# Input statistics of images 1 to 3: from VectorE's bn_stats to ScalarE accumulator passes about the first tile's mean

## The chip, the cores and the metric

The kernel runs on one core of one Trainium2 chip. The metric is device time in microseconds (us) of one execution. The engines are named as in the profile: PE (TensorE; PEld its weight loads), DVE (VectorE), ACT (ScalarE), POOL (GpSimd) and SP (SyncE, which here only issues DMAs). Each engine works through its own instructions in the order in which they were written; between engines, semaphores make one wait for another.

## The reference

Input x has 4 images of 512 channels on 64 x 64 places. Two layers follow each other, each with a group norm (32 groups of 16 channels, statistics over a whole image) ahead of it and a residual around it:

- Layer 0, a Mamba block: a layer norm over channels, the channels cut into 4 chunks of 128, for each chunk projections, a 4-tap convolution, silu, softplus, and a state scan over all 4096 places with 256 inner channels and 16 states, then an output projection, a second layer norm, and a 512 x 512 projection.
- Layer 1, linear attention with 8 heads: relu of queries and keys, key-query products summed over all places, and output projections.

The part that matters here is the mean and variance that the first group norm needs:

```
m = jnp.mean(g, axis=(2, 3, 4), keepdims=True)
s = jnp.var(g, axis=(2, 3, 4), keepdims=True)
return ((g - m) / jnp.sqrt(s + eps)).reshape(v.shape)
```

They take one pass over an image before its first tile can be normed. Per channel the kernel gathers mean and variance, and a small matmul with a matrix of groups (`stats_end`, L344) makes group figures of them.

## The kernel before, in words

An image has 8 tiles of 512 places; a tile holds 4 blocks of 128 channels x 512 places, 1 MB in float32. The main loop goes over 128 steps, one for each image, tile and chunk, and each step has 16 slots: 2 halves of the inner channels, 4 groups of states, and 2 halves of a group. In one slot (`slot`, L741):

- DVE runs two scans (L755), each over 512 places, that read a decay `dA` and an input `bx`.
- ACT computes the decays of later scans (`decay`, L724: one exp each, written to one of three PSUM banks, `LEAD = 3`, so the decay of scan k + 3 waits until scan k is done).
- POOL computes the inputs `bx` of the slot after next (`drive`, L733; three buffers, so it waits for the scans of the slot before).
- In odd slots POOL also copies the last state (L766) and multiplies the last quarter of the states with the output weights (L767); in the following slot DVE does the other three quarters (`product`, L772, traced as L775) and PE sums over states.

Around that, at fixed slots of each step, ACT has bursts: at slot 3 softplus between two loads of activation tables (L1147, L636, L1149), at slot 10 silu between two (L1066, L1067, L1169); and POOL has a gate multiply at slots 1 and 9 and a larger one at slot 4 (L797, L644).

All other work is cut into pieces, Python generators that yield after each piece, and put into four queues. `ahead` holds the norm of the next tile, `late` the end of a finished tile, `rest` the attention of the image before, and `light` the statistics of the next image's input (`input_norm(b + 1)`, added at an image's first step). Image 0's statistics are taken before the loop. At the end of each slot the loop decides what of each queue goes in (L1172 to 1200). `light` gets a turn only in the slots `AWAY = (3, 10)`, or when it waits:

```
if light and light[0][1] == "wait" or s in AWAY and not any(
    q and q[0][1] == "wide" for q in (ahead, late)
):
    one(light)
```

`stats0` (L810) loads a tile of x (names `xs`), then in each turn puts two `bn_stats` on DVE (L816, one per block), so a tile takes one turn for its load and two for its blocks. At the end four `bn_aggr` (L341) give mean and variance. `one` (L1076) lets a queue's next piece run if the word that it yielded is among those allowed in this slot.

Tiles of x, of the finished layer 0 and of attention share three buffers of 1 MB (`TILES = 3`); whoever wants one while all are held yields "wait". Loads are issued on SP's queue, together with all rows that the scans need.

The second group norm's statistics are already gathered in the manner that the change brings: `shifted` (L559) takes bn_stats of the first tile, and for the 7 others lets ACT pass over each block twice (L575), Identity with the negative mean of the first tile as bias, and Square with the same bias, each with an accumulator that sums the outputs; `shifted_end` (L581) makes mean and variance of the sums. Each pass writes its full output to a buffer that nobody reads.

Of the kernel before, what the change touches and what calls it, by code (L numbers as in the profile page):

```python
# [10 lines left out]
AF = mybir.ActivationFunctionType  # L11
# [13 lines left out]
def kernel(  # L25
# [311 lines left out]
    def aggregate(stats, name):  # L337

        mv = small.tile([P, NC, 2], F32, tag="mv", name=f"mv_{name}", bufs=4)
        for c in range(NC):  # L340
            nc.vector.bn_aggr(mv[:, c, :], stats[:, c, :, :].rearrange("p t s -> p (t s)"))  # L341
        return mv

    def stats_end(mv, name):  # L344

        yield from room()
        pm = work_bank(f"pm_{name}")
        mm(pm[:, 0:NC], grp, mv[:, :, 0], start=True, stop=True)
        yield from pause(1)
        ngm = small.tile([P, NC], F32, tag="ngm", name=f"ngm_{name}", bufs=4)  # L350
        nc.vector.tensor_scalar(ngm, pm[:, 0:NC], -1.0, None, ALU.mult)
        d = pm[:, 2 * NC : 3 * NC]
        nc.vector.tensor_tensor(d, mv[:, :, 0], pm[:, 0:NC], ALU.subtract)
        dev = small.tile([P, NC], F32, tag="dev", name=f"dev_{name}")
        nc.vector.tensor_tensor(dev, mv[:, :, 0], pm[:, 0:NC], ALU.subtract)
        nc.vector.tensor_tensor(d, dev, d, ALU.mult)
        nc.vector.tensor_tensor(dev, d, mv[:, :, 1], ALU.add)
        pv = pm[:, NC : 2 * NC]
        mm(pv, grp, dev, start=True, stop=True)
        yield from pause(1)  # L360
        gr = small.tile([P, NC], F32, tag="gr", name=f"gr_{name}", bufs=4)
        nc.vector.tensor_scalar(gr, pv, 1e-5, None, ALU.add)
        free()
        nc.gpsimd.tensor_tensor(gr, gr, mhalf, ALU.pow)
        off = small.tile([P, NC], F32, tag="off", name=f"off_{name}", bufs=4)
        nc.gpsimd.tensor_tensor(off, ngm, gr, ALU.mult)
        return gr, off, ngm
# [439 lines left out]
    def with_skip(f, xn, c):  # L807
        nc.scalar.copy(xn[:, c, NTAP - 1 : NTAP - 1 + T], f["po"])

    def stats0(stats, b):  # L810

        for t in range(NT):
            xt = yield from load_x(b, t, "s")
            yield
            for c in range(NC):
                nc.vector.bn_stats(stats[:, c, t, :], xt[:, c, :])  # L816
                if c == NC - 1:
                    later(1, free_x)
                if c % 2:
                    yield "wait" if c == NC - 1 else None  # L820
# [213 lines left out]

    def input_norm(b):
        stats = stats_tile(f"st0_{b}")
        yield from stats0(stats, b)
        norms[b] = yield from stats_end(aggregate(stats, f"a{b}"), f"a{b}")
        yield

    def tile_norm(b, t):
# [34 lines left out]
    def one(queue, may=ANYWHERE):  # L1076

        while queue:  # L1080
            if queue[0][1] not in (None, "wait", "more", "free") and queue[0][1] not in may:
                return False
            queue[0][1] = next(queue[0][0], queue)
            if queue[0][1] is not queue:
                return queue[0][1] != "wait"
            queue.pop(0)
        return False
# [26 lines left out]
    with tc.manual_schedule():  # L1114
        credit, seen, mix, held[0], held_x[0] = 0.0, work["mm"], iter(()), 0, 0
        for n, (b, t, c) in enumerate(steps):
            f, nm = fs[n], names[n]
            before = fs[n - 1] if n else None
            nxt = fs[n + 1] if n + 1 < N else None
            front = step_inputs(n + 2) if n + 2 < N else iter(())  # L1120
            last_mix, mix = mix, mixers(fs[n + 2], names[n + 2]) if n + 2 < N else iter(())
            if c == 0 and (t + 1 < NT or b + 1 < B):
                add_to(ahead, tile_norm(b, t + 1) if t + 1 < NT else tile_norm(b + 1, 0))
            if c == 0 and t == 0 and b + 1 < B:
                add_to(light, input_norm(b + 1))
            assert c != 2 or not ahead
            for s in range(SLOTS):
                def after():
                    nonlocal credit, seen
                    now[0] = n * SLOTS + s  # L1130
                    for what in [w for at, w in due if at <= now[0]]:
                        what()
                    due[:] = [d for d in due if d[0] > now[0]]
                    if s == 0 and before is not None:
                        take_y(before, n - 1, 1)
                    if s == SLOTS // 2:
                        take_y(f, n, 0)
                    if s < 2:
                        next(last_mix, None)
                    if s < 4:  # L1140
                        spread(f, 1, nm, s)
                    if s == 1 and before is not None:
                        gate(before, 1)
                    if s == 2 and nxt is not None:
                        time_banks(nxt, names[n + 1])
                    if s == 3 and nxt is not None:
                        nc.scalar.preload_act_table_set("softplus")  # L1147
                        time_steps(nxt, names[n + 1])
                        nc.scalar.preload_act_table_set("natural_log_exp_and_others")  # L1149
                    if s == 6 and before is not None:  # L1150
                        pb_, pt_, pc_ = steps[n - 1]
                        with_skip(before, xn[pb_, pt_], pc_)
                        if pc_ == NC - 1:
                            add_to(late, leave(pb_, pt_))
                    if s in (3, 5, 6, 7, 8, 9):
                        next(front, None)
                    if s == 4 and nxt is not None:
                        to_rows(nxt, 0, names[n + 1])
                        to_rows(nxt, 1, names[n + 1])
                    if s == 4 and before is not None:  # L1160
                        pb_, pt_, pc_ = steps[n - 1]
                        out_proj(before, xn[pb_, pt_], pc_, names[n - 1])
                    if s == 9:
                        gate(f, 0)
                    if 8 <= s < 12 and nxt is not None:
                        spread(nxt, 0, names[n + 1], s - 8)
                    if s == 10 and n + 2 < N:
                        silu(n + 2)
                        nc.scalar.preload_act_table_set("natural_log_exp_and_others")  # L1169
                    if s >= 12:  # L1170
                        next(mix, None)
                    may = [  # L1172
                        what for k, what in ((0, "wide"), (1, "one ahead"), (2, "two ahead"))
                        if any(a - 2 * k <= s <= a - k for a in AWAY) or (k == 2 and s == SLOTS - 1)
                    ]
                    if light and light[0][1] == "wait" or s in AWAY and not any(
                        q and q[0][1] == "wide" for q in (ahead, late)
                    ):
                        one(light)

                    limit[0] = 1 if 0 < s < 6 else 2
                    credit = min(credit + 3.5 - (work["mm"] - seen), 2.6)
                    busy = False
                    for queue in (ahead, late, rest):
                        kind = queue[0][1] if queue else None
                        if queue is ahead or kind == "free" or credit > 0 or kind == "more" and not busy:
                            start = work["mm"]
                            one(queue, ANYWHERE if queue is ahead and (c, s) > (1, 4) else may)
                            credit -= work["mm"] - start
                            busy = busy or work["mm"] - start > 1  # L1190
                    if s - 1 in AWAY:
                        for queue in (ahead, late, rest):
                            if queue and queue[0][1] == "free":
                                one(queue)
                    seen = work["mm"]

                slot(n * SLOTS + s, N * SLOTS, after)
            fs[n - 1].clear() if n else None
        product(N * SLOTS - 1)
        fold_states(N * SLOTS - 1, N * SLOTS)  # L1200
        now[0] = None
        for _, what in due:
            what()
# [60 lines left out]
```

## Time and profile before

| what | value |
|---|---|
| median of 3 runs | 7839.31 us (7833.92 to 7841.01) |
| the profiled execution's own time | 7841.1 us |
| its span, first to last instruction | 7839.4 us |
| busy in the span: DVE, POOL | 6905.7 us, 6898.4 us (88% each) |
| busy in the span: PE, ACT | 6444.4 us (82%), 5461.7 us (70%) |
| bn_stats of x (L816) | 128, 81.1 us busy, 32 of them before the loop |
| accumulator passes already there (L575) | 224 and as many reads of the accumulator |

The loop runs from 121 to 7364 us of the span; what follows is the last image's attention, mainly on PE. A busy share is a mean over stages with different limits, so it doesn't tell what a shorter stretch of work is worth: for that one looks at what each engine waits for at that place. In the chain of work that ended last, a step goes back from each instruction to what released it. In the lists of waits, a wait for several things is put down to the one that came last.

### The profile page before, as it was taken

What the parts mean: (1) busy time and instruction counts of PE and PEld (TensorE: products, weight loads), DVE (VectorE), ACT (ScalarE), POOL (GpSimd) and SP (SyncE); (2) the same over time, 40 slices, a digit from 0 to 9 for tenths busy, and PEclk for the clock granted to TensorE, in tenths of its full rate; (3) what the DMA queues carried; (4) which work ended last, traced back from release to release, by engine and by line L of the source; (5) the groups of instructions that cost most, each with busy time, mean ns of one, the idle gap of its engine ahead of it and who ended that gap; (6) DMA issues with size and microseconds to landing.
All of it is one profiled execution on the core that took longest, in us unless ns stands there. A gap on an engine that the chain in (4) does not pass through costs nothing.

```text
span 7839.4 us, 90421 instructions
## 1 busy us (share of the span) xinstructions
PE 6444.4 (82%) x24839; PEld 2099.0 (27%) x24880; DVE 6905.7 (88%) x5650; ACT 5461.7 (70%) x8329; POOL 6898.4 (88%) x4649
## 2 busy tenths in 40 slices
PE   5677777677789888988788888898788888989599
PEld 1121212112223222322222223332222222323144
DVE  5999999999999999999999999999999999999500
ACT  4677777777777777777777777777777777777421
POOL 4999999999999999999999999999999999999500
PEclk7888878888899999998899999999899999999799
DMA  5666666666666656776666666676666666586302
GB/s 164 165 172 168 158 150 162 162 157 169 174 179 169 159 159 159 192 197 169 174 166 169 167 162 160 171 190 183 164 160 168 157 162 154 148 212 182 100 33 91
DMA packets 829184, 1265.87 MB, mean 161 GB/s; under 512 B 183912, under 2 KB 317560, under 8 KB 816384
## 3 DMA queue, kind: packets, MB, share of 16 engines
q1 hardware_dynamic: 804736, 1222.32, 59.6%
q0 software_dynamic: 16896, 33.56, 2.5%
q8 instruction: 195, 3.19, 0.2%
q10 hardware_dynamic: 7040, 4.20, 0.2%
q14 instruction: 317, 2.60, 0.1%
HBM read 1052.78 MB, written 206.57 MB: 161 GB/s over the span
## 4 chain that ended last, share of the span: by engine, by line
DVE 33%; PE 31%; ACT 10%; issue 8%; DMA 7%; POOL 7%; SPq 3%; POOLq 0%; DVEq 0%; ACTq 0%
DVE h L755 21%; DVE h L775 10%; PE pq L129 6%; PE y L129 6%; PE pc L129 5%; POOL bx L737 5%; ACT dA L729 4%; DMA d_all<-d_rows 3%; PE pr L129 3%; PE po L129 2%; SPq L704 2%; PE pp L129 2%; DMA c_sb<-c_rows 2%; PE pd L129 1%; DMA b_all<-b_rows 1%
## 5 line engine op out<-in xcount | busy, mean ns | idle before, releaser
L737 POOL TENSOR_TENSOR bx<-d_all,b_all 128x1024 f32<-128x1024 f32 x2048 | 4824.0, 2367 | 198.2 <-DVE h L755 178.6
L755 DVE TENSOR_TENSOR_SCAN h<-dA,st,bx 128x512 f32<-128x512 f32 x3584 | 4355.5, 1265 | 292.5 <-PE y L129 101.8
L729 ACT ACTIVATE dA<-d_all,a_t 128x512 f32<-128x512 f32 x4096 | 2759.0, 688 | 1491.5 <-DVE h L755 1434.8
L775 DVE TENSOR_TENSOR h<-h,c_all 128x1536 f32<-128x1536 f32 x1024 | 1768.6, 1727 | 0.1
L767 POOL TENSOR_TENSOR h<-h,c_sb 128x512 f32<-128x512 f32 x1024 | 1299.8, 1269 | 99.1 <-DMA c_sb<-c_rows 13.0
L129 PE MATMUL y<-h,fold 128*32 128x512 f32 x8192 | 1264.0, 693 | 45.7 <-POOL h L767 42.4
L129 PE MATMUL c_all<-parts,sel 128*128 128x384 bf16 x1024 | 369.4, 361 | 1021.9 <-DVE h L775 1020.7
L129 PE MATMUL pc<-xn,w_cv 128*128 128x512 f32 x2048 | 1036.6, 639 | 126.0 <-DVE xn L421 62.2
L129 PE MATMUL pq<-w_qk,xa 128*128 128x512 f32 x2048 | 962.5, 602 | 6.7 <-issue 4.1
L755 DVE TENSOR_TENSOR_SCAN h<-dA,bx 128x512 f32<-128x512 f32 x512 | 590.1, 1204 | 76.6 <-ACT dA L729 46.5
L129 PEld LDWEIGHTS pc<-xn,w_cv 128*128 128x128 f32 x2048 | 386.4, 199 | 735.6 <-issue 409.3
L129 PEld LDWEIGHTS <-sel 128*128 128x128 bf16 x1280 | 126.8, 99 | 1668.0 <-DVE h L775 1453.4
L129 PEld LDWEIGHTS pq<-w_qk,xa 128*128 128x128 f32 x2048 | 395.7, 195 | 437.4 <-issue 421.7
L129 PE MATMUL pp<-xn,w_pr 128*128 128x512 f32 x1024 | 478.0, 597 | 3.8 <-DVE xn L421 3.8
L129 PE MATMUL pr<-xb,m 128*128 128x512 f32 x1024 | 476.1, 603 | 4.8 <-POOL m L992 2.2
L129 PE MATMUL y<-xz,dg 32*32 32x512 f32 x2048 | 362.1, 785 | 0.0
L129 PEld LDWEIGHTS y<-h,fold 128*32 128x32 f32 x8192 | 170.5, 114 | 639.7 <-issue 398.1
L848 ACT ACTIVATE kq<-pq 128x512 f32<-128x512 f32 x256 | 150.8, 589 | 265.5 <-PE pq L129 264.8
L797 POOL TENSOR_TENSOR xz<-xz 128x512 f32<-128x512 f32 x256 | 325.1, 1270 | 10.2 <-ACT xz L794 9.3
L644 POOL TENSOR_TENSOR dt<-dt,xz 128x1024 f32<-128x1024 f32 x128 | 302.1, 2360 | 21.4 <-ACT dt L636 21.4
L855 DVE TENSOR_TENSOR kq<-pk,kq 128x256 f32<-128x256 f32 x124 | 51.2, 413 | 277.9 <-PE pk L129 277.7
L129 PE MATMUL pd<-xz,w_xp 128*128 128x512 f32 x512 | 289.3, 692 | 5.2 <-ACT xz L1066 5.2
(178 smaller groups left out, 6164.7 us busy)
## 6 DMA issues: line engine op xcount, KB each, us to landing
d_all<-d_rows SPq DMA_DIRECT2D x2048, 256.0 KB, 4.3
b_all<-b_rows SPq DMA_DIRECT2D x4096, 64.0 KB, 2.3
d_rows<-dt SPq DMA_DIRECT2D x256, 512.0 KB, 2.7
c_sb<-c_rows SPq DMA_DIRECT2D x4096, 16.0 KB, 3.5
xs<-in_x_dram SPq DMA_DIRECT2D x32, 1024.0 KB, 7.8
xn<-in_x_dram SPq DMA_DIRECT2D x32, 1024.0 KB, 8.4
xr<-in_x_dram POOLq DMA_DIRECT2D x32, 1024.0 KB, 10.2
x<-xr SPq DMA_DIRECT2D x32, 1024.0 KB, 4.5
```

Source lines behind the costliest of these rows:

```text
L129: nc.tensor.matmul(out_, lhsT, rhs, **how)
L644: nc.gpsimd.tensor_tensor(f["both"][:, 1], f["both"][:, 0], f["xz"][:, 0], ALU.mult)
L704: nc.sync.dma_start(dst[k * BLK : (k + 1) * BLK, :], rows_[q * KS + k, :].partition_broadcast(BLK))
L729: nc.scalar.activation(dAs[k], fs[n]["d_all", e][:, 0, j, :], AF.Exp, scale=a_t[:, e, j, q : q + 1])
L737: nc.gpsimd.tensor_tensor(bxs[g], fs[n]["d_all", e][:, 1, jj * 2 : jj * 2 + 2, :], bc(b_all[g // JJ], 2), ALU.mult)
L755: nc.vector.tensor_tensor_scan(h[:, j, :], dAs.pop(2 * g + i), bxs[g][:, i, :], 0.0 if t == 0 else st[:, c, e, q, j : j + 1], ALU.mult, AL ...
L767: nc.gpsimd.tensor_tensor(h[:, :, CUT:], h[:, :, CUT:], bc(c_sb.pop(g // JJ), NJ), ALU.mult)
L775: nc.vector.tensor_tensor(own, own, bc(c_all.pop(g // JJ), NJ), ALU.mult)
L797: nc.gpsimd.tensor_tensor(f["xz"][:, 1, e, :], f["xz"][:, 1, e, :], f["xz"][:, 0, e, :], ALU.mult)
L848: nc.scalar.activation(qk[i], pq, AF.Relu)
L855: nc.vector.tensor_tensor(kq, pk, kq, ALU.add)
```

## The change

For images 1 to 3 a new `stats_by_act` takes the place of `stats0`. The first tile still gets one bn_stats per block, whose mean and variance seed the sums. For the other seven tiles each block gets two ACT passes: Identity with the negative mean of the first tile as bias, written back in place, and Square of what that wrote, again in place; each with an accumulator output. `shifted_end`, which was there already, makes mean and variance of the sums. All small results live in the tile that held the bn_stats.

A block is one piece, and yields the word "row". The loop no longer gives such a piece a turn in the slots 3 and 10, but in slots 0, 2, 8 and 14, one block in each. Loads of a tile keep the old turns.

```diff
+    def stats_by_act(stats, b):
...
+        for t in range(NT):
+            xt = yield from load_x(b, t, "s")
+            yield "row"
+            for c in range(NC):
+                if t == 0:
+                    nc.vector.bn_stats(first[:, c, :], xt[:, c, :])
+                    if c == NC - 1:
+                        for o in range(NC):
+                            nc.vector.bn_aggr(mv[:, o, :], first[:, o, :])
+                        nc.scalar.activation(off[:, :, 0], mv[:, :, 0], AF.Copy, scale=-1.0)
+                        nc.vector.memset(sums[:, :, 0:1], 0.0)
+                        nc.scalar.activation(squares[:, :, 0], mv[:, :, 1], AF.Copy, scale=float(T))
+                else:
+                    nc.scalar.activation(
+                        xt[:, c, :], xt[:, c, :], AF.Identity, bias=off[:, c, :],
+                        accum_out=sums[:, c, t : t + 1],
+                    )
+                    nc.scalar.activation(
+                        xt[:, c, :], xt[:, c, :], AF.Square, accum_out=squares[:, c, t : t + 1]
+                    )
+                if c == NC - 1:
+                    later(1, free_x)
+                yield "row" if c < NC - 1 else None
+        return {"sum": sums, "square": squares, "mv": mv}
...
     def input_norm(b):
         stats = stats_tile(f"st0_{b}")
-        yield from stats0(stats, b)
-        norms[b] = yield from stats_end(aggregate(stats, f"a{b}"), f"a{b}")
+        if b:
+            sums = yield from stats_by_act(stats, b)
+            mv = shifted_end(sums, f"a{b}")
+        else:
+            yield from stats0(stats, b)
+            mv = aggregate(stats, f"a{b}")
+        norms[b] = yield from stats_end(mv, f"a{b}")
         yield
...
-                    if light and light[0][1] == "wait" or s in AWAY and not any(
+                    turn = light and light[0][1]
+                    if turn == "wait" or turn != "row" and s in AWAY and not any(
                         q and q[0][1] == "wide" for q in (ahead, late)
                     ):
                         one(light)
+                    elif turn == "row" and s in (0, 2, 8, 14):
+                        one(light, ("row",))
```

## The prediction

> **What bounds the kernel now.** I read the busy times first, then the groups, then the waits, then stretches of equal work, and last one step engine by engine.
>
> The page's first part, and the groups (line, engine, operation, output<-inputs, count | busy us, mean ns | idle us before, releaser):
>
> ```profile
> PE 6444.4 (82%) x24839; PEld 2099.0 (27%) x24880; DVE 6905.7 (88%) x5650; ACT 5461.7 (70%) x8329; POOL 6898.4 (88%) x4649
> ...
> L737 POOL TENSOR_TENSOR bx<-d_all,b_all 128x1024 f32<-128x1024 f32 x2048 | 4824.0, 2367 | 198.2 <-DVE h L755 178.6
> L755 DVE TENSOR_TENSOR_SCAN h<-dA,st,bx 128x512 f32<-128x512 f32 x3584 | 4355.5, 1265 | 292.5 <-PE y L129 101.8
> L729 ACT ACTIVATE dA<-d_all,a_t 128x512 f32<-128x512 f32 x4096 | 2759.0, 688 | 1491.5 <-DVE h L755 1434.8
> ```
>
> DVE and POOL are equally busy; ACT idles 1491 us ahead of its dA, nearly all of it waiting for a scan to free a bank. So ACT has time, but in pieces. The waits (who for whom, us, times, longest) show that DVE and POOL seldom wait long for each other:
>
> ```profile
> POOL bx L737 <- DVE h L755: 178.6, 296, 3.4
> POOL st L766 <- DVE h L755: 58.1, 61, 4.5
> ...
> DVE h L755 <- ACT dA L729: 140.4, 103, 44.5
> ```
>
> Next, steps 1 to 13 of images 1, 2 and 3, bounded by the starts of their scans. Images 1 and 2 hold 32 of the bn_stats each, image 3 none; scans, tile norms and attention of the image before are the same in all. First all engines, then L816 alone:
>
> ```profile
> 1926.00:2667.30 741.30, 631.69 (x2557) 204.00 (x2563) 712.24 (x608) 552.75 (x842) 700.71 (x474) 0.93 0.67 171
> 3754.80:4500.40 745.60, 637.87 (x2557) 206.21 (x2563) 711.95 (x609) 553.00 (x842) 700.23 (x474) 0.92 0.66 170
> 5587.80:6334.80 747.00, 629.85 (x2560) 205.15 (x2566) 693.50 (x567) 552.85 (x841) 700.04 (x472) 0.93 0.63 160
> ...
> 1926.00:2667.30 741.30, 20.34 (x32) 0.93 0.67 171
> 5587.80:6334.80 747.00, 0.00 (x0) 0.93 0.63 160
> ```
>
> (Columns: length, busy us and count of PE, PEld, DVE, ACT, POOL.) Image 3 has 18.5 us less on DVE and is not shorter: the time went into waits. In image 0 (172 to 773 us) DVE is busy 592 and POOL 589 of 601 us. The loop hangs on both engines by turns: by the starts of copy L766 and of bx, POOL is 1 to 3 us behind DVE from slot 3 to about 8 (gate, dt), and in most steps of images 1 to 3 has caught up at slots 13 to 1.
>
> **The Trainium skill.** "ScalarE: Activation LUTs", section What ACT_TABLE_LOAD costs: an ACTIVATE with a pointer bias takes 280 + 0.833 N ns, 707 at N = 512; following ones overlap by 93 ns. The trace has 704 to 733 ns for L575, the same form, and starts 0.63 us apart. "Perfetto Trace Analysis", section Optimizing Scalar/DVE Operations: if DVE is saturated, moving work to Scalar may make sense; its section Optimization Strategy says that the contended engine can change over time. The windows agree with the second; whether the first applies is the question here.
>
> **The change, part by part.**
> *DVE.* Three images times 7 tiles times 4 blocks are 84 bn_stats fewer. Each lasts 0.677 us, but a pair holds the engine for 1.20 (261.90 to 263.09 below), so 84 x 0.60 = 50 us. bn_aggr: 12 of 0.315 become 12 of 0.149 (minus 2.0); six reduces of 0.17 and small work add 1.2. Net minus 51 us.
> *ACT.* 84 blocks. L575's two passes and their accumulator reads run 2526.98 to 2528.40 before the next dA, 1.42 us. Here the Square reads what Identity wrote and waits for its end, about 0.08 more, since a dependent pair (L414, L415) has 0.03 us between end and start: 1.5 us, 126 in all. Bounds: 1.42 with no such wait, 1.8 with nothing overlapped (0.71 + 0.19, twice).
> *POOL.* The end of the sums adds 0.25 + 3 x 0.20 = 0.85 us per image, 2.5 in all, on an engine that is 98% busy in image 0 (589 of 601 us).
> *SP.* The same 24 loads of 1 MB, now mostly at slot 10, once a step. They land in 5.6 to 11.8 us; the first block is at slot 14, about 13 us later. Nothing else in the queue is added; d_all's spreads share the wires with it, as before. Cost nothing; if a load came later, all of ACT's queue, dA first, would stand behind the block.
> *PE.* Nothing. Pieces of attention in steps 1 to 13 of images 1 and 2 move by some slots, because the tile buffers change hands earlier.
>
> *Blocks at slots 0, 2 and 14 (63).* Behind them ACT idles for DVE: 1.9 us in slot 1, 2.1 in slot 3, 1.4 and 1.1 in slots 14 and 15 (means over the steps). Walking each block down ACT's queue until idle time has used it up, and comparing with the scan that takes each dA, 0.3 us in all is late at slot 14, nothing at slot 0, 3.8 at slot 2, where softplus and two table loads follow. POOL is behind there. I take plus 2.
>
> *Blocks at slot 8 (21).* Step 2, ACT, then DVE, then POOL; the block goes in after the second line:
>
> ```profile
> 256.54 0.67 ACT L606 ACTIVATE xz<-pc,cb 128x512 f32<-128x512 f32 x1
> 257.11 0.57 ACT L794 COPY xz<-y 128x512 f32<-128x512 f32 x1
> 257.58 1.31 ACT L729 ACTIVATE dA<-d_all,a_t 128x512 f32<-128x512 f32 x2
> 258.81 0.59 ACT L623 COPY xz<-pz 128x512 f32<-128x512 f32 x1
> ...
> 260.25 1.73 DVE L775 TENSOR_TENSOR h<-h,c_all 128x1536 f32<-128x1536 f32 x1
> 261.90 1.28 DVE L816 BATCH_NORM_STATS2 st<-xs 128x6 f32<-128x512 f32 x2
> 263.09 3.59 DVE L755 TENSOR_TENSOR_SCAN h<-dA,bx 128x512 f32<-128x512 f32 x3
> ...
> 262.94 4.67 POOL L737 TENSOR_TENSOR bx<-d_all,b_all 128x1024 f32<-128x1024 f32 x2
> ```
>
> The dA of 257.58 moves to 259.08 and is done at 259.77, so the scan that started at 259.14 starts 0.7 later and the product at 260.9 ends at 262.7. The pair of bn_stats is gone, so slot 11 starts at 262.6, 0.5 earlier. Slot 12 needs bx, which POOL ends at 265.3, so it starts at 265.4 against 265.46. The block's 1.5 is paid by the pair's 1.2 and by slack. The other 20 go the same way; at the end of their steps DVE stands from 0.9 us early to 1.2 late (steps 5 and 9, where a pair goes and no block comes, counted in): plus 4.6 us summed. About half is met by a POOL that is behind anyway: plus 2.5.
>
> *The 19 pairs removed at slot 3.* DVE's 1.2 us are mostly gone by slot 8, where it waits for POOL or PE: minus 3, between 0 and minus 10.
>
> Sum: 2 + 2.5 - 3 + 2.5 = plus 4. The profiled execution took 7841.1 (span 7839.4 and 1.7 around it), so 7845; the median shown is 1.8 below it, so 7843.
>
> **The rivals.** What a measurement of this kernel can tell from no change is 0.2%, 15.7 us.
> *DVE is the bound where it counts (faster).* For it: from slot 9 to slot 1 POOL's copy often follows the scan at once. If all 29 pairs at slot 10 pay 1.2 (34.8), the 12 first-tile bn_stats in other slots cost 7.2 and POOL 2.5, the gain is 25: 7814. Against: image 3's 747 us, and the silu burst after slot 10 (1.28 + 1.48 + 0.58 + 1.28), which a pair covers.
> *The silu burst comes late (slower).* A slot-8 block pushes the dA behind that burst. With the scans kept at their places, 21 blocks make dA 0.92 us late on average: 19.3, slot 2 adds 3.8 and POOL 2.5: plus 26, 7867. It decides once the missing pair no longer pays, that is, where DVE's early time at slot 10 is lost to POOL. Against: about 2526 us, two L575 blocks stand ahead of the burst and DVE shows no idle time, under a pair and a kq.
> *Only the order of attention changes.* The same work took 741 and 745.6 us in images 1 and 2, so 4 us an image, 8 in all, of either sign; this fills the first case's own range.
> That the change doesn't act is excluded: in the built order, all 84 pairs stand at slots 0, 2, 8 and 14.
>
> **How the numbers follow.** Balance 0.57, 7843, own range 7828 to 7858 (attention's 8, and 1.42 or 1.8 us for a block). Faster 0.26 at 7814. Slower 0.17 at 7867. The range runs from 7808 to 7868: it takes in both rivals and leaves some 0.1 on each side for more. Faster, within and slower have the same chances as the cases.
>
> **What would show it.** Right: bn_stats of xs fall from 128 to 44 with DVE's busy time some 50 us lower; two new ACT groups of 84 at 0.71 us each with reads of 0.19; DVE's idle time before L755 up by about as much as its work fell; POOL's idle time hardly moved. Wrong if POOL's idle for DVE falls by 20 us or more (faster), or if DVE's wait for ACT dA in slots 10 to 12 grows by over 20 (slower); and if the Square starts over 0.3 us after Identity's read, the block is mis-sized.

## The result, and the profile after

The changed kernel takes 7862.95 us (median of 8 executions, 7855.59 to 7871.39) against 7840.16 for the kernel before (median of 8, 7833.92 to 7846.71). The ratio is 1.0027, 95% interval 1.0018 to 1.0037: slower, by 21 us at this ratio. The forecast was no change, 7843, with 7867 for the slower rival.

First the busy times and the groups of the profile after (group columns as before: count | busy us, mean ns | idle us before, releaser):

```profile
PE 6462.9 (82%) x24880; PEld 2106.5 (27%) x24880; DVE 6862.0 (87%) x5575; ACT 5570.6 (71%) x8671; POOL 6901.0 (88%) x4661
...
L737 POOL TENSOR_TENSOR bx<-d_all,b_all 128x1024 f32<-128x1024 f32 x2048 | 4824.5, 2367 | 200.1 <-DVE h L755 182.8
L755 DVE TENSOR_TENSOR_SCAN h<-dA,st,bx 128x512 f32<-128x512 f32 x3584 | 4359.1, 1264 | 331.8 <-ACT dA L729 118.3
L729 ACT ACTIVATE dA<-d_all,a_t 128x512 f32<-128x512 f32 x4096 | 2749.4, 687 | 1387.1 <-DVE h L755 1339.2
```

DVE works 44 us less than before (6905.7) and stands idle ahead of these scans 39 us more (331.8 against 292.5), and 13 us more ahead of the 512 scans of each image's first tile, which are a group of their own (89.7 against 76.6). So all that was taken off it became waiting, and some more.

The new work, in the groups with each shape apart:

```profile
L832 ACT ACTIVATE xs<-xs,st 128x512 f32<-128x512 f32 x84 | 60.5, 720 | 0.4
L836 ACT ACTIVATE xs<-xs 128x512 f32<-128x512 f32 x84 | 52.9, 630 | 2.6
L832 ACT ACTIVATION_READ_ACCUMULATOR xs<-xs,st 128x1 f32 x84 | 16.0, 190 | 0.0
...
L850 DVE BATCH_NORM_STATS2 st<-xs 128x6 f32<-128x512 f32 x32 | 20.1, 680 | 0.1
L824 DVE BATCH_NORM_STATS2 st<-xs 128x6 f32<-128x512 f32 x12 | 8.0, 665 | 0.0
```

And one block as it lies in ACT's queue (start us, length us):

```profile
231.71 0.71 ACT L832 ACTIVATE xs<-xs,st 128x512 f32<-128x512 f32 x1
232.32 0.19 ACT L832 ACTIVATION_READ_ACCUMULATOR xs<-xs,st 128x1 f32 x1
232.54 0.63 ACT L836 ACTIVATE xs<-xs 128x512 f32<-128x512 f32 x1
233.08 0.19 ACT L836 ACTIVATION_READ_ACCUMULATOR xs<-xs 128x1 f32 x1
233.17 1.28 ACT L729 ACTIVATE dA<-d_all,a_t 128x512 f32<-128x512 f32 x2
```

The next dA starts 1.46 us after the block does; over all 84 blocks the median from a block's start to ACT's next instruction is 1.475. The waits (us, times, longest):

```profile
DVE h L755 <- ACT dA L729: 174.3, 145, 44.5
DVE h L755 <- PE y L129: 140.6, 137, 3.2
...
POOL bx L737 <- DVE h L755: 182.8, 298, 3.4
...
POOL st L766 <- DVE h L755: 61.4, 60, 4.8
```

DVE waits 34 us more for ACT's dA (140.4 before) and 24 us more for PE's y (116.5 before); the single wait of 44.5 us stands in both kernels ahead of the loop. POOL's idle time for DVE hardly moved (178.6 and 58.1 before).

Last the same steps as before, 1 to 13 of images 1, 2 and 3 (length, busy us and count of PE, PEld, DVE, ACT, POOL; the granted clock is the third figure from the end):

```profile
1935.94:2683.00 747.06, 632.93 (x2560) 205.21 (x2561) 697.03 (x582) 589.88 (x957) 702.91 (x480) 0.93 0.67 169
3771.92:4519.35 747.43, 632.08 (x2560) 205.76 (x2561) 696.82 (x581) 589.66 (x957) 703.08 (x480) 0.93 0.67 169
5608.35:6355.32 746.97, 630.26 (x2565) 205.23 (x2566) 693.32 (x566) 552.85 (x841) 700.07 (x472) 0.93 0.64 160
```

Images 1 and 2 lost 15 us of DVE's work and gained 37 of ACT's, and took 747 us where they took 741.3 and 745.6. Image 3, which has no such work, took 747.0 in both. From the start of the first scan to the end of the last the loop takes 7259.4 us against 7242.8 before. The work ahead of it and after it is the same in both; in these two profiles the first scan starts at 124.7 and 120.8 us, which is 4 of the 21 us between their spans.

### The profile page after: what moved, and what is told of

The parts are those of the page before. It is cut to its first block, busy times and chain, and to the rows that moved or that the text cites. A ratio compares the mean times of both kernels' runs of the same rounds, so it can differ in the third digit from the quotient of the medians.

```text
span 7860.0 us, 90717 instructions
## 1 busy us (share of the span) xinstructions
PE 6462.9 (82%) x24880; PEld 2106.5 (27%) x24880; DVE 6862.0 (87%) x5575; ACT 5570.6 (71%) x8671; POOL 6901.0 (88%) x4661
## 4 chain that ended last, share of the span: by engine, by line
PE 32%; DVE 31%; ACT 12%; DMA 7%; issue 7%; POOL 7%; SPq 2%; POOLq 0%; DVEq 0%; ACTq 0%
DVE h L755 20%; DVE h L775 10%; PE y L129 6%; PE pq L129 6%; PE pc L129 6%; POOL bx L737 5%; ACT dA L729 4%; PE pr L129 3%; DMA d_all<-d_rows 3%; PE po L129 3%; PE pp L129 2%; DMA c_sb<-c_rows 2%; SPq L704 2%; PE c_all L129 1%; DVE xn L421 1%
## 5 line engine op out<-in xcount | busy, mean ns | idle before, releaser
L755 DVE TENSOR_TENSOR_SCAN h<-dA,st,bx 128x512 f32<-128x512 f32 x3584 | 4359.1, 1264 | 331.8 <-ACT dA L729 118.3
L129 PE MATMUL y<-h,fold 128*32 128x512 f32 x8192 | 1260.6, 691 | 41.3 <-POOL h L767 37.4
L755 DVE TENSOR_TENSOR_SCAN h<-dA,bx 128x512 f32<-128x512 f32 x512 | 591.4, 1203 | 89.7 <-ACT dA L729 56.0
```

What stands on the lines that cost most here:

```text
L129: nc.tensor.matmul(out_, lhsT, rhs, **how)
L755: nc.vector.tensor_tensor_scan(h[:, j, :], dAs.pop(2 * g + i), bxs[g][:, i, :], 0.0 if t == 0 else st[:, c, e, q, j : j + 1], ALU.mult, AL ...
```

## The experiments

Three things happen at once in the change: bn_stats leave DVE, passes enter ACT, and the order of everything in the queues moves, since blocks now take one slot each, a tile is loaded and given back at other places, and pieces of the norm and of attention that wait for a tile buffer move with it. The experiments take these apart. All ratios are to the kernel before on the same chip, with 95% intervals; "loop" is the span of the scans in one profiled execution, which moves by some us between executions. "Clock" is the share of full TensorE clock that was granted over an execution, as the median of a run's executions; it turns out to matter.

| run | order | passes on ACT | us, median | ratio | clock | loop us |
|---|---|---|---|---|---|---|
| before | before | none (bn_stats) | 7837 to 7841 | | 0.906 | 7242.8 |
| after | new | 0, 2, 8, 14 | 7862.95 | 1.0027 [1.0018, 1.0037] | 0.9065 | 7259.4 |
| e1_no_passes | new | left out | 7855.10 | 1.0020 [1.0013, 1.0028] | 0.903 | 7263.5 |
| e2_without_8 | new, slots 0, 2, 14 | 0, 2, 14 | 7856.97 | 1.0028 [1.0017, 1.0038] | 0.903 | 7263.6 |
| e3_without_2 | new, slots 0, 8, 14 | 0, 8, 14 | 7899.26 | 1.0083 [1.0066, 1.0099] | 0.9005 | 7283.5 |
| e4_slots_0_14 | new, slots 0, 14 | 0, 14 | 7845.86 | 1.0011 [1.0002, 1.0020] | 0.905 | 7245.8 |
| e5_bn_out | before | left out | 7841.25 | 1.0001 [0.9993, 1.0010] | 0.906 | 7242.7 |
| e6_bn_in_rows | new | none (bn_stats, one a slot) | 7878.59 | 1.0054 [1.0037, 1.0070] | 0.9025 | 7273.0 |
| e7_before_turns | before | 0, 2, 8, 14 (5 at 10) | 7880.13 | 1.0048 [1.0033, 1.0063] | 0.9035 | 7280.1 |
| e8_passes_at_away | before | two at a time at 3, 10 | 7916.57 | 1.0099 [1.0084, 1.0114] | 0.902 | 7319.3 |
| e9_no_first_tile | new | left out, first tile too | 7848.01 | 1.0016 [1.0009, 1.0022] | 0.904 | 7239.4 |
| e10_no_loads | new | as e9, loads of x too | 7852.48 | 1.0020 [1.0010, 1.0030] | 0.902 | 7252.7 |
| e11_third_pass | new | three a block | 7880.25 | 1.0060 [1.0047, 1.0073] | 0.906 | 7287.0 |
| e12_before_turns_not_8 | before | 0, 2, 14 | 7842.92 | 1.0005 [0.9996, 1.0013] | 0.907 | 7245.8 |

### The passes left out, and other sets of slots

e1 keeps the new order, with the first tile's bn_stats, and issues no passes:

```diff
                 else:
-                    nc.scalar.activation(
-                        xt[:, c, :], xt[:, c, :], AF.Identity, bias=off[:, c, :],
-                        accum_out=sums[:, c, t : t + 1],
-                    )
-                    nc.scalar.activation(
-                        xt[:, c, :], xt[:, c, :], AF.Square, accum_out=squares[:, c, t : t + 1]
-                    )
+                    pass
```

> The changed kernel with its 84 pairs of ACT passes left out (tiles are still loaded and held for the same turns; the statistics of images 1 to 3 are then those of their first tile). Measure: the loop, from the start of the first scan to the end of the last, 7242.8 us before and 7259.4 after. Theory A, the bn_stats on DVE were worth little and the ACT passes cost: the loop is 0 to 10 us shorter than before, so the passes cost 17 to 27. Theory B, the removal pays well and the passes cost still more: 20 to 40 us shorter than before. Theory C, the passes are not the cause, but the moved loads and pieces of attention are: the loop stays 8 us or more longer than before.

The ratio stays at 1.0020. Without a single pass, 124 us of ACT's queue, three quarters of the loss are there. That it is the same loss doesn't follow: e1's executions had a lower granted clock (0.903) than those of the kernel before and of the changed kernel. "What in the order costs" comes back to this.

e2, e3 and e4 change the list of slots:

```diff
-                    elif turn == "row" and s in (0, 2, 8, 14):
+                    elif turn == "row" and s in (0, 2, 14):
```

(`(0, 8, 14)` in e3, `(0, 14)` in e4.)

> Blocks in slots 0, 2 and 14 only, so that a tile takes longer and the passes last to step 16. If the blocks at slot 8, ahead of the silu burst, cost most (theory A1): the loop falls to within 4 us of before. If those at slot 2, ahead of the softplus burst, do (A2): it stays 12 us or more longer, and slot 5 still grows by 12 or more in sum. C: unchanged from the changed kernel within 4 us.

> Blocks in slots 0, 8 and 14 only. A1: the loop stays 10 us or more longer than before, slot 11 grows as in the changed kernel. A2: it falls to within 4 us of before and slot 5 no longer grows. C: unchanged from the changed kernel within 4 us.

> Blocks in slots 0 and 14 only, in 14 steps of each image. If both early slots are to blame and the rest is hidden (A): the loop is 0 to 10 us shorter than before, as without any passes. If passes cost wherever they are put (84 times a share of 1.5 us): as long as the changed kernel, within 4 us.

Without slot 8 the time is the same as with it, without slot 2 it is 0.56% longer (a step then has three slots, so tiles are held longer), and with slots 0 and 14 alone it comes closest to the kernel before, but isn't below it. If each slot had a price of its own, taking slot 2 away could not cost 44 us. So these runs show that a list of slots is also a choice of order, and can't be read as a price list. The clock differs too: e2 and e3 have 0.903 and 0.9005.

### The bn_stats left out, in the order before

e5 is the kernel before, with the bn_stats of tiles 1 to 7 left out in images 1 to 3; PE, ACT, POOL and SP have before's instructions in before's order.

```diff
-                nc.vector.bn_stats(stats[:, c, t, :], xt[:, c, :])
+                if t == 0 or b == 0:
+                    nc.vector.bn_stats(stats[:, c, t, :], xt[:, c, :])
```

> The kernel before with the bn_stats of tiles 1 to 7 of images 1 to 3 left out and nothing else changed (statistics of those images from their first tile alone): every load and every piece of attention stays where it was. Loop before: 7242.8 us; without passes but in the changed order: 7263.5. Theory M, the moved loads and pieces of attention cost: the loop is 7235 to 7246, so removal pays next to nothing and the new order costs the 20 us. Theory R, taking the bn_stats away itself costs, since DVE then runs into other waits: 7255 or more. Rival of both, removal pays and the order costs twice as much: under 7225.

The ratio is 1.0001, at most 0.07% faster. In the same stretches of images 1 and 2:

```profile
1926.10:2665.75 739.65, 635.35 (x2562) 205.69 (x2563) 696.76 (x581) 552.11 (x842) 700.81 (x474) 0.92 0.68 171
3754.63:4495.30 740.67, 635.33 (x2562) 205.89 (x2563) 696.81 (x581) 552.41 (x842) 699.53 (x474) 0.92 0.68 171
```

and in the groups of its page:

```profile
L755 DVE TENSOR_TENSOR_SCAN h<-dA,st,bx 128x512 f32<-128x512 f32 x3584 | 4363.7, 1270 | 317.8 <-ACT dA L729 105.3
```

DVE's work falls by 15 us in each, and the stretches by 1.6 and 4.9. Summed over all steps, and with a slot running from one scan start to the next pair's, slots 3 and 10 get 12.4 and 28.4 us shorter, as they must, and slots 5, 7, 11 and 12 get 14.0, 5.4, 14.6 and 5.4 longer: the next slots in which DVE waits for POOL, ACT or PE take it back. In this order nothing was to be gained on DVE.

### The new order with bn_stats

e6 has the new order, and one bn_stats per block in place of the passes, as many as before in all.

```diff
+                nc.vector.bn_stats(stats[:, c, t, :], xt[:, c, :])
-            sums = yield from stats_by_act(stats, b)
-            mv = shifted_end(sums, f"a{b}")
+            yield from stats_by_act(stats, b)
+            mv = aggregate(stats, f"a{b}")
```

> The changed kernel's order, with one bn_stats on DVE in place of each block's two ACT passes. M: the loop is 7255 to 7275, as long as or longer than the changed kernel, since the order is the same and DVE has its work back at slots 0, 2, 8 and 14. R: at most 7248, since the bn_stats are back. If passes at ACT were what costs: at most 7248 as well.

It takes 1.0054. Slots 0, 2, 8 and 14 are 14.5, 12.6, 14.9 and 13.7 us longer than in the kernel before, for 24 bn_stats each: at 0.60 us, 14.4 us, the whole of it. In these slots DVE sets the pace, and a bn_stats costs what it lasts; in slots 3 and 10, where the kernel before puts it, it costs nothing (e5). That holds for the change too, since it keeps the first tile's 12.

### The passes in the order before

e7 keeps before's loads, its giving back of tiles and PE's and SP's order, and puts the passes at the same slots as the change; five blocks that had no slot in time stand at slot 10.

```diff
+                    elif blocks and s in (0, 2, 8, 14) and blocks[0][0] <= now[0]:
+                        _, what, k = blocks.pop(0)
+                        what(k)
```

> The changed kernel's passes in slots 0, 2, 8 and 14 (five of 84 blocks at slot 10), with the loads and the release of the tiles in the turns of before, so that the loads and all of PE's work stand as before. M: the loop is 7240 to 7250, within 4 us of the kernel without bn_stats in that order plus at most 7 for the passes. If the passes cost by themselves (the 2.5 and 2 us of the prediction were too small): 7255 or more.

e8 puts two blocks at a time where the pairs of bn_stats stood, at slots 3 and 10:

```diff
-            yield "row"
+            yield
...
-                yield "row" if c < NC - 1 else None
+                if c % 2:
+                    yield "wait" if c == NC - 1 else None
```

> The passes in the old turns, two blocks at a time in slots 3 and 10, ahead of the softplus and the silu burst; loads and PE's work stand as before. If ACT's passes are hidden wherever they are: 7240 to 7250. If a block ahead of a burst makes dA late, as the prediction's rival says: two blocks are 3 us each time, 42 times, of which at least a quarter shows: 7275 or more.

Here the passes do cost: 37 us in e7 over e5 (1.0048 over 1.0001), 77 in e8. Against e5, slot 5 is 19.0 us longer in e7 and slot 10 16.7, the slots behind those with blocks at 2 and 8. In e8 slot 5 is 31.6 longer and slot 12 35.0.

e12 is e7 without the blocks at slots 8 and 10:

```diff
                         _, what, k = blocks.pop(0)
-                        what(k)
+                        if s != 8:
+                            what(k)
```

> The order before with passes at slots 0, 2, 14 alone: the 21 blocks at slot 8 and the 5 at slot 10, ahead of and behind the silu burst, are left out, so their statistics are missing. With all 84 blocks this order took 7880, with none 7841. If half of the 37 us is the silu burst coming late (17 us by the slots 10 to 12 of the trace): 7861 to 7865. If slot 2 ahead of softplus carries all: 7878. If slot 8 carries all: 7843.

The time is back at 1.0005: without these 26 blocks 34 of the 37 us are gone. Of the 34.3 us between the two loops, 15.9 are in slot 10 and 3.9 in slot 11. Another 11.0 are in slot 5, which has the same blocks ahead of it in both; there the granted clock, 0.9035 in e7 and 0.907 in e12, may have its part. One of the blocks, at step 11 of image 1, in ACT's queue of e7, and the scan that waits (the timelines of ACT and DVE):

```profile
2542.56 0.67 ACT L606 ACTIVATE xz<-pc,cb 128x512 f32<-128x512 f32 x1
2543.13 0.57 ACT L794 COPY xz<-y 128x512 f32<-128x512 f32 x1
2543.59 0.73 ACT L825 ACTIVATE xs<-xs,st 128x512 f32<-128x512 f32 x1
...
2544.45 0.63 ACT L829 ACTIVATE xs<-xs 128x512 f32<-128x512 f32 x1
...
2545.08 0.71 ACT L575 ACTIVATE sum<-xr,moff 128x512 f32<-128x512 f32 x1
...
2546.49 1.28 ACT L729 ACTIVATE dA<-d_all,a_t 128x512 f32<-128x512 f32 x2
```

```profile
2544.47 1.28 DVE L755 TENSOR_TENSOR_SCAN h<-dA,st,bx 128x512 f32<-128x512 f32 x1
2547.19 1.28 DVE L755 TENSOR_TENSOR_SCAN h<-dA,st,bx 128x512 f32<-128x512 f32 x1 [1.44 <-ACT dA L729]
```

and the same place in e12:

```profile
2526.37 0.73 ACT L575 ACTIVATE sum<-xr,moff 128x512 f32<-128x512 f32 x1
...
2527.79 1.29 ACT L729 ACTIVATE dA<-d_all,a_t 128x512 f32<-128x512 f32 x2
```

```profile
2527.26 2.53 DVE L755 TENSOR_TENSOR_SCAN h<-dA,st,bx 128x512 f32<-128x512 f32 x2
```

Here the end of a tile already puts an accumulator block (L575) between the xz copy and the two dA. With it alone the scan of slot 10 follows at once; with a second block ahead of it the scan waits 1.44 us, the block's whole length. In steps 1 to 13 of image 1 seven blocks stand at slot 8, and slot 10 is longer in e7 than in e12 by 0, 0.5, 1.4, 0.5, 1.4, 1.5 and 0.5 us. The 1.4 to 1.5 are this step and two in which the xz copy (L794) ahead of the block waits 0.95 and 2.2 us for PE's y. A late y alone doesn't decide it: in the first and the fourth of the seven the copy waits 0.81 and 1.12 us, and slot 10 grows by 0 and 0.5. What a block costs differs from step to step, and in the step shown it is another block that has used up ACT's lead. The mean, 0.83 us, is near the 0.92 that the slower rival had worked out. In the step shown it is paid at the second scan of slot 10, by the two dA right behind the block, ahead of the silu burst and its table load.

### A third pass

e11 is the changed kernel, with one more accumulator pass in each block.

```diff
+                    nc.scalar.activation(
+                        xt[:, c, :], xt[:, c, :], AF.Identity,
+                        accum_out=squares[:, c, t : t + 1],
+                    )
                     nc.scalar.activation(
                         xt[:, c, :], xt[:, c, :], AF.Identity, bias=off[:, c, :],
```

> The changed kernel with a third accumulator pass in every one of the 84 blocks (an Identity in place, about 0.72 us each, 60 us of ACT more). If the passes are hidden in this order, as the small step from no passes to two says: not over 10 us above the changed kernel, 7863 to 7873. If they cost as in the order before (37 us for 126 us of ACT): 18 us more, 7881. If each us of ACT ahead of the bursts counts in full at slots 2 and 8 (42 x 0.72): 30 us more, 7893.

It takes 1.0060, 0.33% or 26 us over the changed kernel. The third pass costs 26 us at a like clock (0.906 and 0.9065), close to the 30 of the expectation that counts every us at slots 2 and 8. The first two passes of a block add 5 us to e1's median (1.0027 over 1.0020, the intervals overlap), but at a higher clock than e1 had. Slot 5 is 17.9 us longer and slot 10 13.4. The stretches and the waits of e11:

```profile
1935.47:2696.90 761.43, 641.13 (x2560) 206.57 (x2561) 697.65 (x582) 609.80 (x1013) 703.77 (x479) 0.92 0.65 166
3784.13:4540.14 756.01, 638.16 (x2560) 205.79 (x2561) 697.48 (x581) 609.29 (x1013) 703.23 (x480) 0.92 0.65 167
...
DVE h L755 <- ACT dA L729: 198.9, 151, 44.5
```

The third pass is paid where e7's blocks are, behind slots 2 and 8. In the changed kernel, too, slot 10 is 17.2 us longer than in e1; but slot 11 is 17.8 us shorter. The new order has a wait in slot 11 of its own (in e1 it is 15.4 us longer than in e5), and the late slot 10 runs into that wait. In e7, which lacks it, slot 11 gives nothing back.

### What in the order costs

e9 is e1 without the first tile's bn_stats and bn_aggr; e10 is e9 without the loads of x. All other instructions keep their order on every engine.

```diff
-                    nc.vector.bn_stats(first[:, c, :], xt[:, c, :])
                     if c == NC - 1:
-                        for o in range(NC):
-                            nc.vector.bn_aggr(mv[:, o, :], first[:, o, :])
+                        nc.vector.memset(mv, 1.0)
```

```diff
-            xt = yield from load_x(b, t, "s")
+            while no_tile():
+                yield "wait"
+            held_x[0] += 1
             yield "row"
```

> The new order without the passes (7855 against 7837 before), and now also without the first tile's 12 bn_stats and 12 bn_aggr: one small memset stands where they stood, so no statistics of x are taken in images 1 to 3 at all. Every other instruction keeps its place on every engine. Theory A, the 12 single bn_stats in slots 8, 14, 0 and 2 are what the new order costs: back to 7842 or less. Theories B (the loads of x at slot 10) and C (the shifted order of the norm's and attention's pieces on PE): 12 x 0.6 = 7 us at most come back, 7848 to 7855.

> The kernel of e9 with the 24 loads of x for images 1 to 3 left out as well; the tile buffers are still taken and given back at the same places, so all other engines keep e9's order. Theory B, the loads' new place in SP's queue and on the wires costs time: 10 us or more below e9. Theory C, the order of the pieces: within 4 us of e9, and the loop still some 15 us above that of the order before.

The first tile gives back little: 1.0016 for 1.0020, with overlapping intervals. Its own slots 0, 2, 8 and 14 are 8.2 us shorter in e9 than in e1, about what its 12 bn_stats at 0.60 to 0.68 and the bn_aggr take, so it does pay there; whether all of that reaches the end is not settled. Without the loads the ratio doesn't fall either (1.0020). So a kernel with no statistics of x in its loop and no loads for them is still 0.16 to 0.20% slower in its median than the kernel before, where e5, with as little to do, is not. What remains is the order of the pieces, and what comes with it: a lower granted clock, 0.904 in e9 and 0.902 in e10 against 0.906.

The profiled execution of e9 was shorter than its median (7837.9, the median 7848.0) and that of e10 was at its median (7852.2), and this shows how the clock enters. From image 1, step 5, first e9, then e10, PE's timeline:

```profile
2158.41 1.13 PE L129 MATMUL pt<-dt,w_dt 32*128 32x512 f32 x4
2160.43 1.98 PE L129 MATMUL pc<-xn,w_cv 128*128 128x512 f32 x4 [0.89 <-DVE xn L421]
2162.34 1.06 PE L129 MATMUL mu_sums_b<-xn,ones 128*32 128x512 f32 x8
```

```profile
2163.39 2.08 PE L129 MATMUL pt<-dt,w_dt 32*128 32x512 f32 x4
2166.18 3.78 PE L129 MATMUL pc<-xn,w_cv 128*128 128x512 f32 x4 [0.72 <-DVE xn L421]
2169.89 1.94 PE L129 MATMUL mu_sums_b<-xn,ones 128*32 128x512 f32 x8
```

ACT in e10, and DVE in e9 and e10, some 14 to 17 us later:

```profile
2179.91 0.69 ACT L606 ACTIVATE xz<-pc,cb 128x512 f32<-128x512 f32 x1 [1.64 <-PE pc L129]
```

```profile
2174.27 1.28 DVE L755 TENSOR_TENSOR_SCAN h<-dA,st,bx 128x512 f32<-128x512 f32 x1 [1.15 <-PE y L129]
```

```profile
2182.86 1.28 DVE L755 TENSOR_TENSOR_SCAN h<-dA,st,bx 128x512 f32<-128x512 f32 x1 [2.96 <-ACT kq L877]
```

The granted clock over the four pc (it is the third figure from the end), and over the 3.41 us ahead of the next stretch at half clock in each profile, e9 and then e10:

```profile
2160.43:2162.41 1.98, 1.98 (x8) 1.00 0.41 120
2151.06:2154.47 3.41, 0.58 (x2) 1.00 0.93 209
```

```profile
2166.18:2169.96 3.78, 3.77 (x8) 0.50 0.43 125
2158.57:2161.98 3.41, 1.52 (x13) 1.00 0.60 158
```

The same matmuls in the same order run at half their rate in e10, from pt to mu_sums_b, because half the clock is granted there (2161.98 to 2172.22 us). In e9 the half clock comes earlier and is over before pt (2154.47 to 2157.89). PE's later pieces follow without a pause, so the next pc comes late for ACT, whose copy of it stands ahead of two dA, and the scan waits 2.96 us in place of 1.15. Steps 5 and 9 of images 1 and 2 in all 14 kernels' profiles are 56 such places: where these four pc ran at full rate (0.62 us of busy time each, granted clock 1.00) slot 7 took 3.58 to 3.60 us, where at half rate (1.02 to 1.10 us, clock 0.50 to 0.56) it took 5.06 to 5.39, without exception. At how many of the four places it happens differs: 2 in the kernel before and in the changed one, 4 in e1, e2, e7 and e10, 0 in e5. It is 3.8 us of the 13 between the loops of e9 and e10, 7 of the 21 between e5 and e1, and 5 of the 34 between e12 and e7. It makes no difference between the profiles of before and after.

How far the clock alone moves the time is seen in image 3. All 14 kernels have the same instructions in the same order there, on every engine. Its steps 1 to 13 took 747.0 us in seven of the profiles, all at a granted clock of 0.93, and 748.9 to 751.0 us in the other seven, all at 0.92. The slowest is e5's:

```profile
5583.45:6334.47 751.02, 634.22 (x2565) 206.28 (x2566) 693.84 (x567) 553.08 (x841) 701.10 (x472) 0.92 0.65 159
```

Whole executions show it too: of the 85 of the kernel before in its three series, the 24 with a clock of 0.905 or less took 7840.7 us in the median, the 20 with 0.908 or more 7831.7. Of e9's 21 executions, the seven with 0.903 or less took 7853.7, the four with 0.905 or more 7837.2, which is the time of the kernel before. (A slow execution could also be the cause of a low mean; the 56 places show one way in which the clock comes first.) And e9's profile, with a clock of 0.907, shows no loss from the order in images 1 and 2, though a few us may hide behind the somewhat higher clock:

```profile
1923.02:2662.57 739.55, 628.39 (x2560) 204.23 (x2561) 694.17 (x577) 553.51 (x845) 703.33 (x480) 0.93 0.67 171
3751.54:4492.14 740.60, 631.67 (x2560) 204.37 (x2561) 694.76 (x578) 553.46 (x845) 702.76 (x480) 0.93 0.66 171
```

The changed kernel has PE's order of e9, but not the low clock of e1, e9 and e10. So their 12 to 16 us are not shown to be a part of its 21. From e9's profile to the changed kernel's, images 1 and 2 grow by 7.5 and 6.8 us, at a clock of 0.93 in both. Slot 10 grows by 12.2 us and slot 11 shrinks by 12.7; what is left is mainly slot 5, behind the blocks at slot 2, with 8.7, and slots 0 and 2 themselves with 3.1. Against e1's profile these are 11.8, 12.9, 8.5 and 0.2, so slots 5, 10 and 11 come out alike whatever the clock was. The whole loop grows by 20.0 from e9's, but image 0 has a lower clock in the changed kernel (0.80 against 0.82).

## Where the prediction held and where it failed, step by step

The time was within the range, but on the slower side: +21 where the sum said +4, and 5 us above the likeliest case's own range (7828 to 7858). The range held because it took in the slower rival, whose 7867 was nearest (7865, if its 26 us are added to the median shown, as the faster rival's 25 are taken from it).

- **DVE's work, -51 us, and -3 of it at the end for the pairs at slot 3.** Busy time fell by 44: the bn_stats of x by 53 (81.1 to 28.1), while the scans' busy time rose by 5. The value was nothing: e5 has it at 1.0001. The reading of image 3 (18.5 us less work, no shorter) was right, and was the best single line of the prediction.
- **ACT, 1.5 us a block.** Right: 1.475.
- **Blocks at slots 0, 2, 8 and 14, +2 and +2.5.** By the medians of e1 and the changed kernel right in size, 5 us, but these two differ in clock. By slots the way to it was half right. The blocks at slot 8 do make slot 10 late, by 17.2 us against e1 and 17.6 against e9 over the loop, close to the slower rival's 19.3. What meets it is a wait in slot 11 of the new order, and not the missing pair: in e7 the pair is missing too, and slot 11 gives nothing back. The prediction took the place at about 2526 us, with its two L575 blocks, as evidence that blocks there are free; e7 shows that they use up ACT's lead, so that a block added to them pays 1.44 of 1.475 us. What isn't met is slot 5, behind the blocks at slot 2: 8.5 to 8.7 us in images 1 and 2 alone, where the prediction found 3.8 late in all and took 2.
- **The first tile.** The prediction gave its 12 bn_stats in other slots 7.2 us, but only in the faster rival; the sum of the likeliest case left them out. They lengthen their own slots by 8.2 us in the profiles; in the medians they are worth about 3, within the uncertainty.
- **"Pieces of attention in steps 1 to 13 of images 1 and 2 move by some slots", at nothing, and SP's loads at nothing.** The loads are indeed worth nothing (e10). The order was put at nothing without a reason. Without any statistics it costs 12 to 16 us in the medians, but with a lower granted clock, for which the prediction had no term at all; e9's profile, at 0.907, shows no cost. The rival that spoke of the order allowed 8 us of either sign.
- **POOL, +2.5.** Not measured alone; POOL's busy time rose by 2.6.

Which term holds the 21 us stays open. The medians put 12 to 16 on the order, about 3 on the first tile and about 5 on the passes. That these add up to 20 to 24 proves nothing, for e9, e1 and the changed kernel are one row of differences, and e1 and e9 stand at another clock. The profiles of e9 and the changed kernel put it on the passes and the first tile, and next to nothing on the order; but single profiles of such a loop are uncertain by about 10 us. By the first account the step that failed is the order, put at nothing; by the second it is the blocks at slot 2, taken too small, and the first tile, left out.

Of the signs named ahead, the bn_stats, the groups, POOL's idle time and DVE's growing idle time came as written. DVE's waits for dA in slots 10 to 12 grew from 25.2 to 41.3 us, short of the 20 more that was to speak for the slower rival. Nearly all of it is in slot 10: 8.7 before, 24.6 after, and 9.6 and 8.7 in e1 and e9. So the lateness that this rival described is there, and comes with the passes; slot 11 takes it back.

Open is also why executions of the new order without passes (e1, e9, e10) get a lower clock than those of the changed kernel and of e11. DVE's wait for y is 137.0, 132.7 and 145.9 us in e1, e9 and e10 against 119.7 in e5, but 133.4 in e12 as well, which isn't slow. A run with the new order of blocks and before's order on PE would tell what the order is worth with the passes in; only the kernel with before's order and the passes was run (e7).

## What to carry to other kernels

- Before an engine is relieved, leave the work out at its old place, with everything else kept: here that run (1.0001) says in one step that there is nothing to gain in that order, whatever the busy share of 88% suggests. A stretch of the same loop that lacks the work, like image 3, says it from the profile before.
- Where a scheduler fills slots, a change of turns is a change of order on all engines. It deserves a term of its own, with both signs and a size taken from what equal work takes in different orders, and it has to be measured without the new work, with the granted clock beside each time: two kernels at different clocks differ by more than their order.
- Slack is used once. A block that costs nothing in one step costs its whole length in the next, where another block or a late input has used the lead (0 and 1.44 us here), and two passes that add 5 us to the median of e1 say nothing of the third (26 us).

## What the runs showed of the hardware

- PE has two rates in the same kernel: four pc matmuls of 128x512 took 1.98 or 3.78 us, eight mu_sums_b 1.06 or 1.94, with the same instructions ahead of them, after the same 3.06 to 3.07 us of waiting in slot 2, at a granted clock of 1.00 and 0.50. The Trainium skill, "TensorE: Matmul & The Clock Gate", section Part 1: The HAM clock gate, describes this: the array falls to half its clock after an idle window of about 3.4 us and comes back after a busy one, and the window runs freely, without regard to the kernel. The traces agree in the windows: in all 14 the stretches at half clock last a multiple of 3.41 us, all but the last of each, and the same wait went with a half clock of 3.41 us that began just before its end in e9, and with one of 10.24 us that began 1.5 us after its end in e10. They differ in what idle means: PE was busy for 0.58 and 1.52 us of the 3.41 ahead of these two stretches, and in the loops of the 14 profiles 95% of the 2698 stretches at half clock follow a window in which PE was busy for at most half of the time, only 10% an empty one.
- Which of the two rates falls on a given place changes between kernels with the same order on PE, so a single profile of such a loop is uncertain by about 10 us: the profiled executions of e9 and e10 differ by 14.4 us, their medians by 4.5.
- An accumulator pass that reads what the pass before wrote starts 0.83 to 0.85 us after it; a block of two such passes holds ACT for 1.475 us, three for 2.23, against 1.42 for the two independent passes of L575.
